# A four-layer Mamba and convolution kernel: half 1 of each image taken first, the next image's first steps moved ahead, column matmuls issued in one run, and three smaller edits

## The chip, the cores and the metric

The kernel runs on one core of one Trainium2 chip. Its metric is the device time of one execution in microseconds (us). Before the change the median of three runs is 5528.93 us (5525.22 to 5535.81). The profiled execution took 5550.92 us, with a span of 5548.9 us and a mean granted TensorE clock of 0.898.

Engines are named as in the profile: PE is TensorE (PEld its weight loads), DVE is VectorE, ACT is ScalarE, POOL is GpSimd, SP is the queue engine that issues most loads. Each takes its own instructions in order.

## The reference, cut to what matters

Input and output are `x` of shape (8, 384, 32, 32), float32: eight images, 384 channels, 1024 pixels. Four layers follow each other.

```python
# layer 0, per image (B=8, C=384, L=1024 pixels as a sequence, 16 states per channel)
xn = rmsnorm(x)                                   # over channels
def mamba(x):                                     # once forward, once on the flipped sequence
    u, z  = split(x @ in_proj.T)
    u     = silu(causal_conv1d(u, 4 taps))
    dt, Bm, Cm = split(u @ x_proj.T)
    delta = softplus(dt @ dt_proj.T + b)
    h     = exp(delta*A) * h + delta*u*Bm         # step by step along the sequence
    y     = sum(h * Cm) + u*D
    return (y * silu(z)) @ out_proj.T
g = (mamba(xn) + flip(mamba(flip(xn)))) * scale_mod
x = x + res_scale * (g + sigmoid(dwconv3x3(xn)) * xn)
# layer 1: bn -> 1x1 conv -> dwconv3x3 -> bn -> 1x1 conv, + x          (gives x1)
# q, k, v = 1x1 conv(x1); phi(t) = exp(0.5*(2t - t*t)) on q and k; 8 heads
# kv = k'v; z = 1/(q . sum(k)); out = (q kv) z; proj, + x1             (gives x2)
# layernorm over channels, 384 -> 1536 -> 384 MLP with gelu, + x2
# layers 2 and 3: depthwise convolutions up to 13x13 with folded branches, a 1x1 conv, gelu
```

The change touches layers 0 and 1 only.

## The kernel before, in words

An image's 1024 pixels are handled as two halves `h` of 512, its channels as three chunks of 128 (`c` or `m`). Layers 0 and 1 are written as generators, in `_layers01`:

- `front(b)` is layer 0 up to the scan: load `xi` (L578), squares and norm (`sq`, then `rsqrt_mean` with the matmuls `ms_s`, `ms_b`), `xn` (L585), in-projection (`in`, `uz`), the 3x3 local branch (`lc`, `lg`; the sigmoid is L615, `local` is L617 to L620), the 4-tap convolution (`c`, `uc`), `xd`, and the deltas (`dt`, `dl`, `deltas`), which are stored to DRAM.
- `scan(b)` is the recurrence. It has twelve units: direction `d`, half `h` (0, 1 forward, then 1, 0 backward), chunk `c`. A unit has four rounds `r`. In each round and for each of two pairs of channel groups, ACT makes the decay `da` (L771), DVE makes `du` in PSUM (L776) and runs two scans into `hs` (L788), POOL multiplies `hs` by Cm (L797), and PE sums the states with four 128x32 matmuls, one per strip of 32 output rows (`sums`, L733), two of them from each `hs` tile, into `acc`. At the end of a unit `acc` goes to `yf_d`, or in the backward direction DVE multiplies it by `zr` and POOL stores `g_d` (L745). The last thing stored for an image is thus `g` of half 0.
- `layer1(b)` is layer 1: load `xx` and `g` (L878, L879), out-projection `op` (L885 adds it to `xx`), first 1x1 conv (`h`, `hh`, L893) with a store and a reload of the image, 3x3 conv (`dw`), second 1x1 conv (`c2`, L910 to L917), keys and values (`kp`, `vt`, `kvs`, L929 to L955), queries (`qp`), the normaliser (`den`, `rz`, `rzb`, L1002 to L1020), projection (`pj`), layer norm (`mu`, `ln`, `var`), MLP (`mf` L1055, `hm` L1057, `mo` L1059). `last` (L1065) stores the result to `x2_d`.

The driver at the end steps `scan(b)` 48 times for each image, and between the steps advances `front(b + 1)` and `layer1(b - 1)` so that their yielded costs stay in the proportion 90 to 325 and are used up at the last round (L1087 to L1115). What is left then is run before the next image. After image 7's scan, `layer1(7)` runs alone, and then layers 2 and 3 (`conv`, L282).

The written order is not the final one: a scheduler orders each engine's instructions by priority and by when it expects their inputs, and so may put other instructions between two that stand together in the source. `defer` and `tick` hold back a DVE step by one or more rounds; `force` runs it early (L931).

Full matmuls of 384x128 by 512 go through `dense` (L500). Products with 32 output rows go through `col32` (L507): four matmuls for the four column strips of the array. Shared buffers: seven `a6` tiles (128x3x512: `xi`, `xn`, `uc`, `xx`, `g`, `hh`, `dw`, `qp`, `pj`, `ln`), nine `t2` tiles (128x512), eight `hs`, four `da`, four `w`; in PSUM one `acc`, one `du`, two `mm` (`psum`) and three `mo` (`long_psum`).

Of the kernel before, what the change touches and what calls it, by code (L numbers as in the profile page):

```python
# [1 line left out]

# [12 lines left out]
P = 128  # L15
# [3 lines left out]
W = 32  # L19
# [18 lines left out]
N_REP, N_DA, N_HS = 6, 4, 8  # L38
TP = H * (KP // 2)
# [335 lines left out]
def _layers01(tc, nc, B, xv, x2_d, dram, ident, mean_w, eps5, eps6, one, half, minus1, vec, bns, bnt,  # L375
# [12 lines left out]
    with ExitStack() as ctx:  # L388
# [45 lines left out]
        selt = const(sel, [P, 32], "selt")  # L434
        neg_a = const(alog, [P, NG, NR], "neg_a")
        nc.scalar.activation(neg_a, neg_a, AF.Exp)
        nc.vector.tensor_scalar_mul(neg_a, neg_a, -1.0)
        mask = const(headmask, [PR, PR], "mask")
        m8 = const(mask8.rearrange("(k p) e -> p k e", p=P), [P, NC, 32], "m8")
        nc.scalar.dma_start(wdt[32:64, :], mask8_t)  # L440
# [42 lines left out]
        def defer(n, fn):  # L483
            e = [n, fn]
            late.append(e)
            return e

        def force(e):
            if e in late:
                late.remove(e)  # L490
                e[1]()
# [15 lines left out]
        def col32(ps, lhs, rhs, taps):  # L507

            for i in range(taps):
                for j in range(4):  # L510
                    nc.tensor.matmul(  # L511
                        ps[32 * j : 32 * j + 32, :], lhs(j, i), rhs(j, i),
                        start=(i == 0), stop=(i == taps - 1), skip_group_check=True,
                    )
# [17 lines left out]
        def conv3(t_d, slot, h, c, taps, name, psum=psum):  # L532

            ims = []
            for j in range(4):
                im = sp.tile([P, 18 * (W + 2)], FP, tag="im", name=f"{name}_i{j}", bufs=N_IM)
                src = bass.AP(
                    t_d.tensor, t_d[slot, 32 * (4 * c + j), 16 * h * (W + 2)].offset,
                    [[IMG, 32], [1, 3], [1, 18 * (W + 2) - 2]],
                )  # L540
                nc.sync.dma_start(im[:96, 0 : 18 * (W + 2) - 2], src)
                ims.append(im.rearrange("p (h w) -> p h w", w=W + 2))
# [3 lines left out]
                lambda j, i: ims[j][:96, i : i + 16, 0:W], 3,  # L546
# [25 lines left out]
        def front(b):  # L572

            xn = []
            for h in range(2):
                cols = bass.ts(h, HALF)
                xh = a6(f"xi_{b}_{h}")
                nc.sync.dma_start(xh, xv[b][:, :, cols])  # L578
                sqs = [t2(f"sq_{b}_{c}_{h}") for c in range(NC)]
# [29 lines left out]
            for h in range(2):  # L609
                for c in range(NC):  # L610
# [4 lines left out]
                    nc.scalar.activation(lc, ps, AF.Sigmoid, bias=vec("dw_b0", c))  # L615

                    def local(h=h, c=c, lc=lc, xr=xr):  # L617
                        nc.vector.tensor_mul(rows(lc), rows(lc), xn[h][c])
                        nc.vector.scalar_tensor_tensor(xr, lc, rs, xr, ALU.mult, ALU.add)
# [6 lines left out]
            for h in range(2):  # L626
                cols = bass.ts(h, HALF)
                ucs = [a6(f"uc_{b}_{h}_{d}") for d in range(2)]
                for c in range(NC):
                    uts = []  # L630
                    for j in range(4):
# [5 lines left out]
                        nc.sync.dma_start(ut[:, 0 : HALF + 3], src)  # L637
                        uts.append(ut)
                    for d in range(2):
# [3 lines left out]
                            lambda j, i: uts[j][:, 3 * d : 3 * d + HALF], 1,  # L643
                        )
                        nc.scalar.activation(ucs[d][:, c, :], ps, AF.Silu, bias=vec("conv1d_b", c))  # L645
# [4 lines left out]
                for k in range(NC):  # L650
                    for d in range(2):
                        nc.tensor.matmul(
                            ps[64 * d : 64 * d + 64, :], wx[:, k, :], ucs[d][:, k, :],
                            start=(k == 0), stop=(k == NC - 1), skip_group_check=True,
                        )
# [31 lines left out]
        def scan(b):  # L687
# [36 lines left out]
            def sums(k, r, hs, acc, y0, zt):  # L724
# [7 lines left out]
                for j in range(4):  # L732
                    nc.tensor.matmul(  # L733
                        acc[32 * j : 32 * j + 32, :], selt, hs[j // 2][:, bass.ts(j % 2, HALF)],
                        start=False, stop=(r == NR - 1), skip_group_check=True,
                    )
                if r < NR - 1:
# [12 lines left out]
            for k, (d, h, c) in enumerate(units):  # L750
                cols = bass.ts(h, HALF)
                second = k % (2 * NC) >= NC
                for r in range(NR):
# [9 lines left out]
                    hs = []  # L763
                    way = slice(None) if d == 0 else slice(None, None, -1)
                    end = HALF - 1 if d == 0 else 0
                    for i in range(2):
# [30 lines left out]
                        nc.gpsimd.tensor_mul(  # L797
                            pairs(t), pairs(t), bct[r][:, 1:2, :].to_broadcast([P, 2, HALF])
                        )
                        hs.append(t)  # L800
                    late.append((k, r, hs, acc, y0, zt))
# [70 lines left out]
        def layer1(b):  # L872

            xx = []
            w = wtile(outproj_t, f"wo_{b}")
            for h in range(2):
# [3 lines left out]
                xx.append(xh)  # L880
# [7 lines left out]
            for h in range(2):  # L888
# [17 lines left out]
            res = [[], []]  # L906
            for h in range(2):
                for m in range(NC):
                    ps = long_psum(f"c2_{b}_{m}_{h}")
                    dense(ps, w, m, dws[h])  # L910
                    t = t2(f"c2_{b}_{m}_{h}")
                    nc.scalar.activation(t, ps, AF.Identity, bias=biasc[:, m, :])

                    def residual(o=xx[h][:, m, :], t=t):
                        nc.vector.tensor_add(o, o, t)

                    res[h].append(defer(1, residual))  # L917
# [11 lines left out]
            for t in range(L // P):  # L929
                h, q = divmod(t, HALF // P)  # L930
                for e in res[h]:  # L931
                    force(e)
                pix = xx[h][:, :, q * P : (q + 1) * P]
                kp, vt = t2(f"kp_{b}_{t}"), t2(f"vt_{b}_{t}")
                for w, dst in ((wk, kp), (wv, vt)):
# [7 lines left out]
                    else:  # L943
                        vv1 = vt[:, : C + NPR].rearrange("p (a e) -> p a e", e=PR + 1)
                        nc.gpsimd.memset(vv1[:, :, PR : PR + 1], 1.0)
# [47 lines left out]
            qps, rzs, xns = [], [], []  # L993
# [8 lines left out]
            for h in range(2):  # L1002
                den = long_psum(f"den_{b}_{h}")
                for k in range(NC):
                    nc.tensor.matmul(
                        den[32:64, :], ksv[:, k, :], qps[h][:, k, :], start=(k == 0), stop=(k == NC - 1)
                    )
                rz = t2(f"rz_{b}_{h}")
                nc.scalar.activation(rz[32:64, :], den[32:64, :], AF.Ln, bias=eps6[32:64])
                nc.scalar.activation(rz[32:64, :], rz[32:64, :], AF.Exp, scale=-1.0)  # L1010
                rzs.append(rz)
                yield 3
            for h in range(2):
                for k in range(NC):
                    ps = long_psum(f"rzb_{b}_{h}_{k}")
                    nc.tensor.matmul(
# [192 lines left out]
```

## Time and profile before

| stretch of the span | us | PE busy | DVE busy | ACT busy | POOL busy | clock |
|---|---|---|---|---|---|---|
| scan of image 0 | 192.5 to 671.4 | 298.65 | 423.42 | 288.56 | 330.10 | 0.68 |
| scan of image 1 | 671.4 to 1203.4 | 464.41 | 452.69 | 349.51 | 339.10 | 0.93 |
| scan of image 3 | 1759.3 to 2311.6 | 463.26 | 433.63 | 349.74 | 333.97 | 0.90 |
| scan of image 5 | 2861.5 to 3387.2 | 455.92 | 426.98 | 358.83 | 331.18 | 0.93 |
| scan of image 7 | 3929.9 to 4405.0 | 379.62 | 399.99 | 259.96 | 315.76 | 0.90 |
| layer 1 of image 7, layers 2 and 3 | 4405.0 to 5548.9 | 1045.75 | 161.57 | 173.10 | 176.20 | 0.95 |

Scans end one after another, so an image's stretch is the time from the end of the last scan product of the image before to the end of its own. The front of the next image and layer 1 of the one before run inside it. Busy time is the union of an engine's instructions in the stretch. A row with two busy columns near its length has no room; a row with none has waits.

Groups of instructions that the change touches, from the table of groups by line:

| line | engine, what | count | mean ns |
|---|---|---|---|
| L733 | PE, `acc` sums (two records per matmul) | 3072 | 657 |
| L511 | PE, `dw`, `lc` (two records per matmul) | 1152 each | 611, 656 |
| L615 | ACT, sigmoid | 48 | 688 |
| L618, L619 | DVE, the local branch | 48 each | 1470, 958 |
| L912 | ACT, `c2` bias | 48 | 679 |
| L915 | DVE, residual | 48 | 1006 |
| all | ACT, table loads | 755 | 1283 |

### The profile page before, as it was taken

To read this page: it belongs to the slowest core of one execution; us is meant where nothing else is said; L and a number is where in the kernel's file an instruction comes from. 1 tells how busy PE (TensorE), PEld (TensorE's weight loads), DVE (VectorE), ACT (ScalarE), POOL (GpSimd) and SP (SyncE) were. 2 spreads that over 40 slices of the span, in tenths; PEclk is the share of its full clock that TensorE was granted. 3 is DMA by queue.
4 is the path that set the end of the run, shared out by engine and by line. 5 is a ranking of instruction groups with operands and counts; after the bars stand their busy time and mean duration, and the time that the engine had idled before them with its cause. 6 is when DMAs were issued, how large, how long until landed. Compare 5 with 4: busy or idle time off the path is not lost. (4 is left out here: it accounts for less than half of the span.)

```text
span 5548.9 us, 57079 instructions
## 1 busy us (share of the span) xinstructions
PE 4603.1 (83%) x19360; PEld 2057.3 (37%) x19360; DVE 3614.0 (65%) x3679; ACT 2906.8 (52%) x3902; POOL 2888.6 (52%) x1603
## 2 busy tenths in 40 slices
PE   5665589868996899689978987898698799899899
PEld 1221133323332333233323322333233243697598
DVE  1598997967787778687977896788788601111211
ACT  1565546774686368646774776477546422001211
POOL 3476676646665666555755674567566500110133
PEclk8776699989998999899989998999898899999999
DMA  9755585787578755864565576557644622466676
GB/s 322 236 178 165 185 258 185 213 217 227 187 234 200 232 168 191 190 200 152 196 214 175 158 213 180 179 172 212 171 142 144 110 87 57 109 166 170 185 166 149
DMA packets 528251, 1012.11 MB, mean 182 GB/s; under 512 B 60616, under 2 KB 196248, under 8 KB 527960
## 3 DMA queue, kind: packets, MB, share of 16 engines
q1 hardware_dynamic: 387952, 665.99, 39.6%
q0 software_dynamic: 71136, 248.53, 17.4%
q10 hardware_dynamic: 68872, 93.95, 5.2%
q8 instruction: 154, 2.52, 0.2%
q14 instruction: 137, 1.12, 0.1%
HBM read 763.86 MB, written 288.36 MB: 190 GB/s over the span
## 5 line engine op out<-in xcount | busy, mean ns | idle before, releaser
L797 POOL TENSOR_TENSOR hs<-hs,bct 128x1024 f32<-128x1024 f32 x768 | 2377.3, 3097 | 1078.2 <-DVE hs L788 600.5
L771 ACT ACTIVATE da<-dlt,neg_a 128x512 f32<-128x512 f32 x1536 | 1031.0, 714 | 759.0 <-DVE hs L788 716.1
L788 DVE TENSOR_TENSOR_SCAN hs<-da,carry,du 128x512 f32<-128x512 f32 x768 | 946.5, 1268 | 327.8 <-ACT da L771 161.5
L776 DVE TENSOR_TENSOR du<-vr,bct 128x1024 f32<-128x1024 f32 x768 | 1057.2, 1377 | 85.8 <-DMA vr<-v_d 50.2
L788 DVE TENSOR_TENSOR_SCAN hs<-da,du 128x512 f32<-128x512 f32 x768 | 898.6, 1207 | 80.2 <-ACT da L771 36.2
L733 PE MATMUL acc<-hs,selt 128*32 128x512 f32 x3072 | 668.9, 657 | 263.6 <-POOL hs L797 235.4
L1059 PE MATMUL mo<-hm,w 128*128 128x512 f32 x1152 | 569.4, 636 | 89.5 <-ACT hm L1057 64.0
L502 PE MATMUL mf<-ln,w 128*128 128x512 f32 x1152 | 549.8, 619 | 38.9 <-ACT uc L645 27.9
L771 ACT ACT_TABLE_LOAD x295 | 378.5, 1283 | 21.0 <-issue 7.1
L1059 PEld LDWEIGHTS mo<-hm,w 128*128 128x128 f32 x1152 | 216.1, 198 | 432.2 <-issue 243.5
L733 PEld LDWEIGHTS acc<-hs,selt 128*32 128x32 f32 x3072 | 111.7, 113 | 671.6 <-POOL hs L797 395.5
L502 PEld LDWEIGHTS mf<-ln,w 128*128 128x128 f32 x1152 | 216.7, 196 | 361.6 <-issue 296.5
L502 PE MATMUL in<-xn,win 128*128 128x512 f32 x576 | 295.8, 645 | 27.1 <-ACT phi_k L869 26.0
L316 PE MATMUL cv_b<-xt_b,toep 128*64 128x256 f32 x2688 | 304.7, 388 | 14.2 <-DVE xt_b L298 14.2
L316 PE MATMUL cv_a<-xt_a,toep 128*64 128x256 f32 x2688 | 305.5, 389 | 9.4 <-DVE xt_a L298 9.4
L316 PEld LDWEIGHTS cv_b<-xt_b,toep 128*64 128x64 f32 x2688 | 282.6, 199 | 36.8 <-issue 16.1
L316 PEld LDWEIGHTS cv_a<-xt_a,toep 128*64 128x64 f32 x2688 | 282.7, 199 | 31.9 <-issue 11.2
L502 PE MATMUL op<-g,wo 128*128 128x512 f32 x288 | 151.0, 679 | 160.0 <-issue 90.0
L511 PE MATMUL dw<-dw_i,t3b 96*32 96x512 f32 x1152 | 211.6, 611 | 39.0 <-DMA dw_i<-h_d 38.6
L511 PE MATMUL lc<-lc_i,t 96*32 96x512 f32 x1152 | 199.8, 656 | 38.3 <-issue 29.0
L1057 ACT ACTIVATE hm<-mf,biasf 128x512 f32<-128x512 f32 x192 | 130.9, 687 | 176.9 <-PE mf L502 175.3
L298 DVE COPY xt_b<-xt_b 64x2480 f32<-64x2480 f32 x24 | 38.2, 1594 | 263.1 <-DMA xt_b<-xp_d 263.1
(185 smaller groups left out, 5287.9 us busy)
## 6 DMA issues: line engine op xcount, KB each, us to landing
dlt<-dl_d SPq DMA_DIRECT2D x384, 256.0 KB, 4.4
vr<-v_d SPq DMA_DIRECT2D x384, 256.0 KB, 4.8
bct<-bc_d SPq DMA_DIRECT2D x256, 256.0 KB, 4.3
ut<-u_d SPq DMA_DIRECT2D x192, 257.5 KB, 5.1
lc_i<-xn_d SPq DMA_DIRECT2D x192, 228.8 KB, 5.3
dw_i<-h_d SPq DMA_DIRECT2D x192, 228.8 KB, 4.5
tp_d<-g_d POOLq DMA_DIRECT2D x64, 672.0 KB, 7.1
w<-w_d SPq DMA_DIRECT2D x64, 576.0 KB, 5.6
```

Source lines behind the costliest of these rows:

```text
L298: nc.vector.tensor_copy(half1[:, :, 0 : XL - 1], half0[:, :, 1:XL])
L316: nc.tensor.matmul(ps[2 * H * e : 2 * H * (e + 1), 0:BW], tp[:, 2 * (g % (GB // 2)) + e, :, :, t].rearrange("p c j -> p (c j)"), rhs, star ...
L502: nc.tensor.matmul(ps, w[:, k, m * P : (m + 1) * P], rhs[k] if isinstance(rhs, list) else rhs[:, k, :], start=(k == 0), stop=(k == NC - 1),)
L511: nc.tensor.matmul(ps[32 * j : 32 * j + 32, :], lhs(j, i), rhs(j, i), start=(i == 0), stop=(i == taps - 1), skip_group_check=True,)
L733: nc.tensor.matmul(acc[32 * j : 32 * j + 32, :], selt, hs[j // 2][:, bass.ts(j % 2, HALF)], start=False, stop=(r == NR - 1), skip_group_ch ...
L771: nc.scalar.activation(da[:, bass.ts(j, HALF)], dlt[:, bass.ts(j, HALF)], AF.Exp, scale=neg_a[:, g, r : r + 1],)
L776: nc.vector.tensor_mul(pairs(du), pairs(vt), bct[r][:, 0:1, :].to_broadcast([P, 2, HALF]),)
L788: nc.vector.tensor_tensor_scan(t[:, s][:, way], da[:, s][:, way], du[:, s][:, way], k_c if second else 0.0, ALU.mult, ALU.add,)
L797: nc.gpsimd.tensor_mul(pairs(t), pairs(t), bct[r][:, 1:2, :].to_broadcast([P, 2, HALF]))
L1057: nc.scalar.activation(hm, ps, AF.Gelu, bias=biasf[:, NC * i + f, :])
L1059: nc.tensor.matmul(acc[m], wb[:, f, m * P : (m + 1) * P], hm, start=(i == 0 and f == 0), stop=(i == FF // C - 1 and f == NC - 1),)
```

## The change

1. **Second half first.** `layer1` makes `op` and `h` for half 1 before half 0, since half 1's `g` was finished three units earlier.
2. **First steps ahead.** Eight rounds before the end of an image's scan, four steps of the front after the next (both loads of `x`, norm, `xn`) and one of the coming `layer1` (weights, `xx` and `g` of half 1) are issued. New `yield 0`s make these separate steps. The planner's costs become 100 and 310.
3. **Column products in one run.** `together` gives the products after the first a high priority and keeps them in program order, and ties the first one to everything that the run reads, for the scheduler's order alone.
4. **Residual from PSUM.** DVE adds the `c2` product, its bias and the residual in one operation that reads PSUM; the ACT copy and the held-back addition go, and `force` with it.
5. **Normaliser side by side.** `den` of both halves lies in two column strips of one PSUM tile and `rz` in one tile, so the matmuls of the two halves can run together, and ACT does both logarithms and then both exponentials. `rzb` alternates between the halves.
6. **Sigmoid from tanh.** sigmoid(x) = (1 + tanh(x/2))/2, with the halves folded into `dwh` and `rsh`. DVE's multiply becomes (t + 1) * xn.
7. The ones column of `vt` is copied by ACT from a constant instead of being set by POOL.

```diff
+AHEAD = 5000
...
+        behind = mybir.DependencyInfo(mybir.DependencyClass.NoSync, mybir.DependencyReason.DATA)
+        def together(products, made):
+            for i, product in enumerate(products):
+                if i == 0:
+                    first = product()
+                    for m in made:
+                        tc.add_manual_dep(first.ins, m.ins.name, behind, reason="together")
+                else:
+                    with tc.high_priority(AHEAD):
+                        tc.keep_in_program_order(product())
+        def col32(ps, lhs, rhs, taps, made):
+            together([ ... for i in range(taps) for j in range(4)], made)
...
                 nc.sync.dma_start(xh, xv[b][:, :, cols])
+                yield 0
...
-                    nc.scalar.activation(lc, ps, AF.Sigmoid, bias=vec("dw_b0", c))
+                    nc.scalar.activation(lc, ps, AF.Tanh, bias=dwh[:, c, :], scale=0.5)
                     def local(h=h, c=c, lc=lc, xr=xr):
-                        nc.vector.tensor_mul(rows(lc), rows(lc), xn[h][c])
-                        nc.vector.scalar_tensor_tensor(xr, lc, rs, xr, ALU.mult, ALU.add)
+                        nc.vector.scalar_tensor_tensor(
+                            rows(lc), rows(lc), one, xn[h][c], ALU.add, ALU.mult
+                        )
+                        nc.vector.scalar_tensor_tensor(xr, lc, rsh, xr, ALU.mult, ALU.add)
...
-            def sums(k, r, hs, acc, y0, zt):
+            def sums(k, r, hs, made, acc, y0, zt):
-                for j in range(4):
-                    nc.tensor.matmul(
-                        acc[32 * j : 32 * j + 32, :], selt, hs[j // 2][:, bass.ts(j % 2, HALF)],
+                together([
+                    partial(
+                        nc.tensor.matmul, acc[32 * j : 32 * j + 32, :], selt,
+                        hs[j // 2][:, bass.ts(j % 2, HALF)],
                         start=False, stop=(r == NR - 1), skip_group_check=True,
                     )
+                    for j in range(4)
+                ], made)
...
-            for h in range(2):
+            for h in (1, 0):
                 xh, gh = a6(f"xx_{b}_{h}"), a6(f"g_{b}_{h}")
...
-                    t = t2(f"c2_{b}_{m}_{h}")
-                    nc.scalar.activation(t, ps, AF.Identity, bias=biasc[:, m, :])
-                    def residual(o=xx[h][:, m, :], t=t):
-                        nc.vector.tensor_add(o, o, t)
-                    res[h].append(defer(1, residual))
+                    o = xx[h][:, m, :]
+                    nc.vector.scalar_tensor_tensor(o, ps, biasc[:, m, :], o, ALU.add, ALU.add)
...
-                        nc.gpsimd.memset(vv1[:, :, PR : PR + 1], 1.0)
+                        nc.scalar.copy(vv1[:, :, PR : PR + 1], ones)
...
+            den, rz = long_psum(f"den_{b}"), t2(f"rz_{b}")
+            ats = [slice(32, 64), slice(96, 128)]
+            for k in range(NC):
+                for h, at in enumerate(ats):
                     nc.tensor.matmul(
-                        den[32:64, :], ksv[:, k, :], qps[h][:, k, :], start=(k == 0), stop=(k == NC - 1)
+                        den[at, :], ksv[:, k, :], qps[h][:, k, :], start=(k == 0), stop=(k == NC - 1),
+                        skip_group_check=True,
                     )
...
+            for k in range(NC):
+                for h, at in enumerate(ats):
                     ps = long_psum(f"rzb_{b}_{h}_{k}")
+                    nc.tensor.matmul(ps, wdt[at, bass.ts(k, P)], rz[at, :], start=True, stop=True)
                     nc.vector.tensor_mul(qps[h][:, k, :], qps[h][:, k, :], ps)
-                yield 3
+                yield 1
...
-                work.append([front(b + 1), 90, 0])
+                work.append([fronts[b], 100, 0])
-                work.append([layer1(b - 1), 325, 0])
+                work.append([seconds[b - 1], 310, 0])
...
+                if i == rounds - 8:
+                    for gen, n in ((fronts[b + 1 : b + 2], 4), (seconds[b : b + 1], 1)):
+                        for _ in range(n):
+                            for g in gen:
+                                next(g)
```

## The prediction

> **What bounds the kernel now.** I read the page's busy shares first, then cut the span into the eight images of the scan (an image ends where the last `hs` product of its twelve units ends on POOL), then one image into its units.
>
> ```profile
> PE 4603.1 (83%) x19360; PEld 2057.3 (37%) x19360; DVE 3614.0 (65%) x3679; ACT 2906.8 (52%) x3902; POOL 2888.6 (52%) x1603
> ```
>
> No engine is full, and the shares mix stages. The scan runs from 192.5 to 4405 us; the rest is one lone layer 1 (to 4760 us) and the convolutions, where TensorE is 99% busy and which the diff leaves alone. Image 4 of the scan, one row per unit (columns: length; PE, PEld, DVE, ACT, POOL busy; granted clock; DMA share; GB/s):
>
> ```profile
> 2311.60:2383.80 72.20, 36.84 (x155) 15.23 (x154) 46.58 (x56) 37.01 (x52) 33.85 (x32) 0.76 0.82 188
> 2416.20:2446.70 30.50, 25.82 (x147) 7.40 (x147) 29.16 (x33) 9.92 (x16) 25.49 (x9) 0.94 0.67 199
> 2501.60:2551.80 50.20, 48.06 (x186) 22.55 (x186) 31.86 (x27) 31.01 (x45) 27.11 (x14) 1.00 0.22 76
> 2718.70:2753.60 34.90, 34.90 (x118) 12.51 (x111) 31.89 (x26) 33.06 (x40) 25.86 (x11) 1.00 0.68 226
> 2794.00:2861.50 67.50, 64.45 (x197) 22.88 (x197) 36.72 (x33) 61.26 (x67) 31.37 (x21) 0.99 0.57 194
> ...
> sum 549.90, PE 466.03 PEld 174.40 DVE 432.19 ACT 365.67 POOL 332.95; mean PE 38.84 PEld 14.53 DVE 36.02 ACT 30.47 POOL 27.75
> ```
>
> A unit can't be shorter than DVE's own scan work (30.5 us, unit 2). Some units are bound by DVE, some by PE (4 and 9; unit 11 by PE and ACT together). The first unit is bound by nothing: 72.2 us with DVE at 46.6 and PE at 36.8. The first units of images 1 to 7 last 58.4, 68.8, 72.6, 72.2, 52.6, 69.1 and 59.8 us, mean 64.8. The timeline of PE and SP at that boundary, and the list of waits, say why:
>
> ```profile
> 2323.51 1.13 PE L666 MATMUL dt<-xd,wdt 24*128 24x512 f32 x4
> 2355.64 3.50 PE L502 MATMUL op<-g,wo 128*128 128x512 f32 x4 [31.01 <-issue]
> 2359.07 0.86 PE L555 MATMUL ms_s<-sq,mean_w 128*32 128x128 f32 x24
> 2346.67 0.37 SPq L879 DMA_DIRECT2D g<-g_d  x1
> ```
>
> ```profile
> PE op L502 <- issue: 90.0, 3, 31.0
> PE op L502 <- DMA g<-g_d: 70.1, 5, 32.6
> PE ms_b L564 <- ACT ms_r L561: 62.6, 15, 21.3
> DVE xx L885 <- PE op L502: 105.6, 17, 31.7
> DVE xn L585 <- PE ms_b L564: 65.9, 10, 18.8
> ```
>
> Layer 1 begins with half 0, whose `g` is the last thing the scan writes. PE takes its instructions in order, so the next image's norm matmuls (`ms_s`, `ms_b`) and scan sums queue behind it, and DVE behind those (18.3 us in image 4). Part of the 31 us is the store: `g_d` is issued at 2326.5, after three `x2_d` stores (16.8 us to landing in the page's list of issues), and `g` is loaded only 20 us later.
>
> **What the Trainium skill says.** "TensorEngine Tiling (Array Packing)", Key Properties: "Tiles operate independently". The trace agrees: a complete column group of `acc` (8 records, 4 matmuls) takes 1.06 us, and two of its records alone take 1.02, so a group cut in two pays a second pass. "ScalarE: Activation LUTs", Table sets, puts tanh in the exp set, and the same page prices a load at 1283 ns plus a drain; the trace has 1283 ns, and `da` starts 0.01 us after it, so no drain is added here. "SBUF — State Buffer", SBUF: two separate sides: DVE operations with two SBUF inputs share a port pair with GpSimd and block. The trace agrees: L915 (both inputs in SBUF) has median 691 but mean 1006 ns, while L885 with one input from PSUM has mean 742.
>
> **The change part by part.** Counts come from the instruction order of the two builds, durations from the trace.
>
> *Second half first, and steps ahead.* Half 1's `g` was written by unit 8. In the new order PE has, between the last `acc` product and the first matmul that needs half 0, the last `mo` (2.84), one or two `in` (2.84 each) and `op` of half 1 (3 x 2.84 = 8.5): about 14 us that don't wait for it. In images 1 to 6 the `g_d` store also stands ahead of at least two of the three `x2_d` stores, so it lands after some 4 us instead of 20. From the end of the last `acc`: DVE has about 8 us of scans ahead of `zr`, then issue and landing 5, load 7: 20 us against 14 of work, so about 6 us of PE wait remain instead of 31. The norm of the next image moves eight rounds up, into units 9 to 11. DVE's boundary waits in the scan are 105.6 - 40.9 (in the lone tail) + 65.9 = 130 us; I take 110 as saved. Queued behind the remaining wait: `op` of half 0 and one `acc` group, so DVE can wait for `acc` again; `hs` has eight buffers, two rounds' slack. The a6 tiles limit the move: `g` of half 0 takes the buffer of `ln` of the image before, free once its last `mf` is done, which the new order has ahead of the boundary. The tail after 4405 us: PE waits 28.1 us for `g`; `op` of half 1 now fills 8.5.
>
> *Column products in one run.* Of 384 `acc` groups 222 stood unbroken, now 358. Counted as 0.95 us passes over the order, `acc` needs 502 before and 403 after; `lc` 160 and 145; `dw` 164 and 170; `c`, `xd` 296 and 294. That is 110 passes, and the normaliser's two halves side by side (`den`) save 24 more: 134 x 0.95 = 127 us of PE. In image 4 the units with PE at 95% or more (4, 5, 9, 11) are 197 of 550 us, so I count about 55 us of it (43%, some units being mixed). The cost: the first product is placed only after both `hs` products.
>
> *Residual from PSUM.* Removes 48 ACT operations (0.68 us, 33 us) and a step of the chain; DVE's 48 go from mean 1006 to the 742 of L885: 13 us. PE then waits for DVE to free the bank instead of ACT; `mo` has three, and nothing needs that bank within two `c` groups, so nothing.
>
> *Sigmoid from tanh.* The 43 loads in front of L615 go, and others move: 755 loads become 691, 64 x 1.283 = 82 us of ACT. L618 becomes the form of L619: mean 1470 to 958, 24 us of DVE. ACT is bound only in unit 11, with PE, where I have counted PE: nothing extra. DVE's 13 + 24 = 37 us count in units DVE bounds (1, 2, 6, 7, 8, 10: 225 of 550): 15 us.
>
> *Ones by ACT.* Removes 64 POOL memsets (0.1 us each) that queue behind POOL's 3.1 us products, and adds 64 tiny ACT copies. Nearest row: 243 ns for 128x48 (16 us), at worst the 468 of L946 (30 us), beside an ACT that waits 716 us for DVE. PE waits 37.4 us for `vt` by this tile's answer; I take 10. *rzb order, new constants*: nothing, a dozen small operations at the start, under the first loads.
>
> Sum: 110 + 55 + 15 + 10 + 12 (tail: 8.5 and three `den` passes) = 202. 5528.9 - 202 = 5327.
>
> **The rivals.**
> A, *moved, not removed*. Per unit the new order gives PE 31, 62, 51, 21 us in units 8 to 11, where the same count had 16, 36, 35, 60 before: the pile moves from 11 to 9 and 10. If the wait for `g` stays at 15 us (half of 31) and crowding costs 10 us an image, 202 - 7x8 - 7x10 = 76 are saved: 5450. For it: `g` is still the scan's last product. Against: those 14 us of work.
> B, *PE is the bound throughout*. Then all of 127 counts, with PE's boundary waits: 62 + 70 for `op` and 63 + 49 for `ms_b`, `ms_s` (244), less 6 x 7 left, plus 8.5: 338. 5190. For it: PE is 85% busy in an image. Against: units of 30.5 us bound by DVE.
> C, *slower*. Each group now waits on PE until POOL's second product is done. At half a product (1.55 us) for 384 groups, half of it in units that PE bounds, it costs 298 us: 5327 + 298 = 5625. For it: PE already waits 235.4 us for `hs` at L733. Against: the run is placed after the product, with other matmuls ahead of it.
>
> **How the numbers follow.** Forecast 0.58, A 0.20, B 0.14, C 0.08. The time is the forecast's. The range reaches over A and to just short of B, 5200 to 5470. Faster takes the forecast, A and B less 0.01, same 0.02, slower 0.07.
>
> **What would show it.** First units of images 1 to 7 near 49 us (now 64.8); the PE wait for `op` in the scan down from 132 to about 45 us; unit 11 near 36 us and units 9 and 10 near 60 and 50; PE busy down by about 110 us or more; table loads 691; no DVE wait for ACT's `c2`; images 1 to 6 at 515 to 522 us instead of 526 to 556. It is wrong if the first unit stays above 60 us, if PE's wait for `hs` at the new run grows by over 100 us, or if DVE starts to wait for the loads that stand behind `g` in SP's queue.

## The result, and the profile after

The changed kernel took **5355.93 us** (median of 4 runs, 5353.65 to 5363.4) beside 5532.37 us for the kernel before on the same chip: **0.9685 of before, interval 0.9668 to 0.9702**. The forecast was 5327 us, 29 us too low, with a range of 5200 to 5470. In the profiled executions the span went from 5548.9 to 5351.9 us; the 197 us between them are placed below, and what the forecast's sum got wrong lies inside them.

The page after, first part:

```profile
PE 4510.2 (84%) x19360; PEld 2032.3 (38%) x19360; DVE 3602.4 (67%) x3684; ACT 2796.1 (52%) x3854; POOL 2892.9 (54%) x1539
```

PE's busy time fell by 93 us and ACT's by 111 us, DVE's by 12. Table loads fell from 755 to 691. None of this says where the time came from, so here is image 4 of the scan again, one row per unit (length; PE, PEld, DVE, ACT, POOL busy; clock; DMA share; GB/s). The rows are units 0, 2, 4, 9, 10 and 11:

```profile
2238.00:2285.90 47.90, 37.88 (x104) 14.96 (x97) 44.22 (x49) 20.97 (x32) 25.89 (x18) 0.93 0.81 158
2313.90:2344.30 30.40, 24.45 (x123) 6.04 (x122) 28.21 (x32) 14.21 (x21) 25.40 (x9) 0.83 0.73 222
2398.00:2431.10 33.10, 31.52 (x148) 15.47 (x150) 29.66 (x24) 24.95 (x45) 26.48 (x9) 1.00 0.43 138
2598.80:2656.90 58.10, 53.87 (x164) 19.20 (x168) 37.28 (x33) 49.73 (x56) 30.33 (x19) 0.94 0.59 193
2656.90:2711.20 54.30, 48.70 (x187) 19.69 (x188) 41.74 (x39) 47.98 (x58) 34.88 (x26) 0.91 0.73 221
2711.20:2746.80 35.60, 33.04 (x96) 12.93 (x98) 33.80 (x30) 29.93 (x35) 28.20 (x11) 1.00 0.67 229
```

Unit 0 went from 72.2 to 47.9 us and unit 11 from 67.5 to 35.6, while units 9 and 10 grew from 34.9 and 40.4 to 58.1 and 54.3: PE and ACT are both nearly full in them, which is where unit 11's pile now lies. Unit 4 lost 17 us: PE, which bounded it, has 16.5 us less to do there, in part because work has moved to other units (148 records of PE instead of 186). Unit 2 is DVE's own scan and did not move.

The timeline of PE, POOL and SP at this boundary:

```profile
2244.07 2.74 PE L505 MATMUL in<-xn,win 128*128 128x512 f32 x6
2248.61 7.99 PE L505 MATMUL op<-g,wo 128*128 128x512 f32 x18 [1.80 <-DVE xx L1090]
2263.10 5.29 PE L505 MATMUL op<-g,wo 128*128 128x512 f32 x6 [6.50 <-DMA g<-g_d]
2248.19 0.58 POOL L772 DMA_DIRECT2D g_d<-zr  x1
2250.56 0.36 SPq L907 DMA_DIRECT2D g<-g_d  x1
```

The `x` counts are records, two for each matmul, so x18 is the `op` of one half. Before, PE stood 31.01 us ahead of the `op` of half 0. Now `in` and the `op` of half 1 run in that time, and 6.50 us are left. The store of `g` was issued at 2248.19 and the load could start at 2250.56, 2.4 us later instead of 20. The list of waits after:

```profile
PE op L505 <- DMA g<-g_d: 98.9, 7, 18.5
DVE xx L914 <- PE op L505: 86.4, 11, 22.3
PE ms_b L582 <- ACT ms_r L579: 50.2, 14, 8.7
DVE xn L604 <- PE ms_b L582: 50.3, 15, 16.6
```

98.9 us of waits for `g` remain, 81.2 of them inside the scan (the rest is the lone layer 1 of image 7). The single waits, at the starts of images 2 to 7, are 17.7, 18.3, 6.5, 2.5, 18.5 and 17.7 us: image 4, shown above, is one of the two good boundaries, and image 5 the other.

From here on one table carries most of the reading: mean length of the groups of units over images 1 to 6, in us, cut at the ends of POOL's `hs` products. The last two rows belong to runs that are described further down.

| kernel | unit 0 | 1, 2 | 3 to 5 | 6 to 8 | 9, 10 | 11 | image | image 7 |
|---|---|---|---|---|---|---|---|---|
| before | 65.6 | 62.0 | 136.6 | 135.2 | 78.0 | 65.8 | 543.1 | 475 |
| changed | 47.6 | 63.1 | 126.0 | 128.5 | 112.4 | 36.0 | 513.6 | 453 |
| changed, again (`c_after`) | 50.4 | 63.6 | 125.3 | 129.0 | 115.7 | 36.0 | 520.1 | 459 |
| before, other order (`b_320`) | 69.9 | 61.3 | 137.6 | 138.0 | 110.5 | 37.3 | 554.7 | 471 |

Six images save 29.5 us each (177), image 7 saves 22, and the rest of the span loses 2 (up to the end of image 0 it is 7 us longer, after image 7 it is 5 shorter). Per image, unit 0 gives 18.0, units 3 to 8 give 17.3, units 1 and 2 take 1.1 back and units 9 to 11 together 4.6. These shares are good to some microseconds only: the two profiled executions had mean granted clocks of 0.898 (before) and 0.905. `c_after`, the same changed kernel on another chip at 0.898, saves 23.0 us an image against the same row: unit 0 gives 15.2, units 3 to 8 give 17.5, and units 9 to 11 take 7.9 back.

### The profile page after: what moved, and what is told of

It is laid out like the page before. It is cut to its first block, busy times and chain, and to the rows that moved or that the text cites. A ratio compares the mean times of both kernels' runs of the same rounds, so it can differ in the third digit from the quotient of the medians.

```text
span 5351.9 us, 56759 instructions
## 1 busy us (share of the span) xinstructions
PE 4510.2 (84%) x19360; PEld 2032.3 (38%) x19360; DVE 3602.4 (67%) x3684; ACT 2796.1 (52%) x3854; POOL 2892.9 (54%) x1539
## 5 line engine op out<-in xcount | busy, mean ns | idle before, releaser
L803 DVE TENSOR_TENSOR du<-vr,bct 128x1024 f32<-128x1024 f32 x768 | 1042.9, 1358 | 50.6 <-DMA vr<-v_d 35.7
L522 PE MATMUL acc<-hs,selt 128*32 128x512 f32 x2304 | 588.2, 679 | 149.5 <-POOL hs L824 149.5
L517 PE MATMUL acc<-hs,selt 128*32 128x512 f32 x768 | 440.5, 668 | 81.2 <-POOL hs L824 63.7
L318 PEld LDWEIGHTS cv_b<-xt_b,toep 128*64 128x64 f32 x2688 | 282.7, 199 | 37.2 <-issue 16.6
L1093 POOL DMA_DIRECT2D x_d<-xx x48 | 55.8, 1168 | 352.4 <-DVE xx L1090 351.7
L505 PE MATMUL op<-g,wo 128*128 128x512 f32 x288 | 146.4, 662 | 103.2 <-DMA g<-g_d 98.9
```

The lines of the kernel that those rows point to most:

```text
L318: nc.tensor.matmul(ps[2 * H * e : 2 * H * (e + 1), 0:BW], tp[:, 2 * (g % (GB // 2)) + e, :, :, t].rearrange("p c j -> p (c j)"), rhs, star ...
L505: nc.tensor.matmul(ps, w[:, k, m * P : (m + 1) * P], rhs[k] if isinstance(rhs, list) else rhs[:, k, :], start=(k == 0), stop=(k == NC - 1),)
L517: first = product()
L522: tc.keep_in_program_order(product())
L803: nc.vector.tensor_mul(pairs(du), pairs(vt), bct[r][:, 0:1, :].to_broadcast([P, 2, HALF]),)
L1093: nc.gpsimd.dma_start(x2v[m, :, h * (H // 2) : (h + 1) * (H // 2), PADW + b * (W + PADW) : PADW + b * (W + PADW) + W,], rows(o),)
```

## The experiments

Ratios are to the kernel before, measured beside each run, with 95% intervals. The runs were made on different chips (the kernel before took 5532 us beside the changed kernel, 5561 to 5564 us beside the experiments), so ratios are compared between chips, not times. Where a profile of an experiment is set against the changed kernel on a chip of the same speed, that is `c_after`.

### Undoing the order at the boundary

Half 0 first and nothing ahead (`u_order`), and half 1 first but nothing ahead (`u_ahead`); both return to the old planner's costs. The first two lines, which stand once for `op` and once for `h`, are in `u_order` alone:

```diff
-            for h in (1, 0):
+            for h in range(2):
...
-                work.append([fronts[b], 100, 0])
+                work.append([fronts[b], 90, 0])
-                work.append([seconds[b - 1], 310, 0])
+                work.append([seconds[b - 1], 325, 0])
-                if i == rounds - 8:
-                    for gen, n in ((fronts[b + 1 : b + 2], 4), (seconds[b : b + 1], 1)):
...
```

> The changed kernel with half 0 first again, no steps ahead, and the planner's old costs 90 and 325; all else as changed. Theory (the image boundary was the largest part): the first units of images 1 to 7 go back from a mean of 48 us to 62 or more, PE again idles 25 to 30 us there for g, and the time is 5356 plus 110 to 140, so 5466 to 5496. Rival (the shorter PE work of the column runs carried the gain, and a wait at the boundary is made up for later in the image): under 5400.

> The changed kernel with half 1 still first, but no steps ahead and the planner's old costs. Theory: op of half 1 covers 8.5 us of the wait for g, but its own loads and the next image's norm (ms_s, ms_b with their ACT steps) stand at the boundary again: first units near 57 us, time 5420 to 5450. Rival 1 (the order of the halves alone does it): 5360 to 5375. Rival 2 (half 1 first is worth nothing without the loads ahead): as the kernel with half 0 first, 5466 or more.

Measured: `u_order` **0.9938** (0.992 to 0.9955), `u_ahead` **0.9961** (0.9948 to 0.9974). Most of the gain is gone in both, and they are nearly equal: half 1 first brings nothing that shows by itself. The list of waits of `u_ahead`:

```profile
PE op L505 <- DMA g<-g_d: 87.4, 7, 16.0
DVE xx L914 <- PE op L505: 56.4, 12, 20.3
```

Its wait for `g` is shorter than the changed kernel's, and still its unit 0 lasts 67.9 us (`u_order` 68.6) with DVE busy for 47 of image 4's 74 us. So the turned halves do not empty the first unit without the early steps; whether the early steps would do it without the turned halves wasn't tried. This result does not hang on the drawn order, to which the next sections come: in all runs of this document the kernels without early steps have a mean first unit of 65.6 to 69.9 us (before, `b_320` and these two), and those with them one of 38.9 to 52.7.

The two kernels do not show what the early steps crowd. The early norm does stand in unit 10 of the changed kernel, and units 9 and 10 take 87.7 and 91.7 us together in the two kernels, 112.4 in the changed one, unit 11 62.2 and 60.9 against 36.0. But `b_320`, which has no early steps, has 110.5 and 37.3: another planner's cost alone moves the pile out of unit 11. And units 9 to 11 together take 149.9 and 152.6 us without the early steps, 148.4 with them.

### Undoing the column runs

```diff
-            for i, product in enumerate(products):
-                if i == 0:
-                    first = product()
...
-                    with tc.high_priority(AHEAD):
-                        tc.keep_in_program_order(product())
+            for product in products:
+                product()
```

> The changed kernel with the column products issued one by one in source order, without priority and without the tie to all inputs. By the instruction order 212 of 384 acc groups stand unbroken instead of 358, and PE needs 106 passes of 0.95 us more, 101 us. Theory (43% of them in units that PE bounds): 5356 + 45 to 60, so 5401 to 5416. Rival B (PE is the bound throughout): about 5455. Rival C (the run makes PE wait for hs, and so costs something): under 5356.

Measured: **0.9937** (0.992 to 0.9953). PE is busy for 4631.9 us against 4510.2. Units 3 to 8 take 272.7 us an image instead of 254.5, as they should when PE bounds some of them; unit 0 takes 52.7 us, 5 more than in the changed kernel and 2 more than in `c_after`, with waits for `g` of 137.9 us in all. The direction is that of the forecast; the size is more than twice the 45 to 60 us expected, and not clean, for the reason that the controls give below.

### Undoing the small parts

All four at once (`u_small`: sigmoid, ACT's `c2` copy, ones by POOL, `den` apart), and then the residual (`u_res`), the sigmoid (`u_tanh`) and the pair of `den` and ones (`u_dv`). The edits are the "+" and "-" lines of the change for these parts, turned round; for the residual:

```diff
-                    nc.vector.scalar_tensor_tensor(o, ps, biasc[:, m, :], o, ALU.add, ALU.add)
+                    nc.scalar.activation(t, ps, AF.Identity, bias=biasc[:, m, :])
+                    def residual(o=xx[h][:, m, :], t=t):
+                        nc.vector.tensor_add(o, o, t)
+                    res[h].append(defer(1, residual))
```

> The changed kernel with sigmoid, the ACT copy of c2, POOL's memset of the ones and the separate normalisers back; order, steps ahead and column runs as changed. Theory: 15 (DVE port) + 10 (memset) + 5 (den and rzb) = 30 us more, 5386. Rival (73 more table loads, 94 us of ACT, with 33 us of c2 copies are on the path): 5356 + 60 to 100. Rival (nothing of it is on the path): 5356 within 10.

> The changed kernel with only the ACT copy of c2 and the later addition back. The order of the other instructions stays as it was (9679 of 9682 on PE). ACT gets 48 copies of 0.68 us, and each kv step waits for one more link. Theory of the prediction: DVE's port sharing alone, 5 to 15 us, a ratio to the kernel before of 0.970 to 0.972. Rival (the four small edits are a real 180 us, and this is the one on the path of c2 and kv, where that kernel lost 12 us an image): 0.98 to 0.99.

> The changed kernel with only the sigmoid back: 82 table loads more by the instruction order, 105 us of ACT. Theory of the prediction: ACT has room, only the DVE form counts, 10 us, ratio 0.970. Rival 1 (units 9 and 10 are now bound by PE and ACT together, so table loads count there): 60 to 100 us, ratio 0.979 to 0.986. Rival 2 (any edit makes the scheduler draw another order, worth 1 to 2% either way): like the kernel with only the planner's cost changed.

> The changed kernel with only the normaliser's halves apart again and POOL's memset of the ones: 18 more PE passes (17 us), 64 memsets of 0.1 us on POOL. Theory: 15 to 20 us, ratio 0.971 to 0.972. Rival (another order is drawn, 1390 of PE's 9682 instructions stand elsewhere): over 0.98.

Measured: `u_small` **1.0006** (0.9995 to 1.0017), `u_res` **0.9751** (0.9735 to 0.9766), `u_tanh` **0.9807** (0.9794 to 0.9821), `u_dv` **0.9976** (0.9967 to 0.9984).

`u_small` missed all three of its expectations: the whole gain is gone, though the order of the halves, the early steps and the column runs are in place. Its first units stay short (44.2 us), and the time is lost elsewhere: units 1 to 5 take 210.7 us against 188.9 in `c_after`. `u_dv` has the same pattern (44.9 and 205.4).

`u_res` is the clean one: all but 3 of PE's 9,682 instructions keep their order, and it costs 0.66% (0.51% against `c_after`), some 28 to 37 us, where the forecast had counted about 5 (13 us of DVE at its share of bound units). Its list of waits has

```profile
DVE xx L951 <- ACT c L948: 129.7, 14, 56.6
```

against 126.6 us of waits for PE's `c` in the changed kernel, so the wait only changed its name. The time is in the unit where the `c2` products stand: unit 3 takes 52.7 us in the mean of images 1 to 6 against 49.5 in `c_after`, with ACT busy for 38.1 instead of 29.7 us there in image 4. No other unit differs by more than some 1 us.

`u_tanh` has 773 table loads instead of 691, 105 us of ACT, and pays 1.2% (some 68 us), but not where ACT is short: against `c_after`, units 6 and 8 get 9.1 and 6.0 us longer and units 9 to 11 together 6 shorter. `u_dv` makes no sense as a sum: `den` taking 43.5 us of PE instead of 28.3, and 64 memsets of 0.1 us cannot cost 2.9% (160 us). Together the single undos come to 2.5 (order), 2.5 (runs), 0.7 (residual), 1.2 (sigmoid) and 2.9%, 9.8% in all, for a change that brought 3.15%. Something else moves when one part is taken out.

### The control: the same instructions in another order

```diff
-                work.append([seconds[b - 1], 310, 0])
+                work.append([seconds[b - 1], 305, 0])
```

> A control: the changed kernel with the planner's cost for layer 1 at 305 instead of 310, and nothing else. The same instructions, in another order (1476 of PE's 9682 stand elsewhere), PE passes 4485 instead of 4482. Theory (what counts is the work and the moves at the boundary, not the drawn order): ratio 0.967 to 0.972. Rival (the time depends on the drawn order as much as on any one edit): outside 0.962 to 0.977.

Measured: **0.9587** (0.9572 to 0.9602), a point better than the changed kernel and outside the band. One planner's cost decides between the two: the list of instructions is that of the changed kernel (but for 702 table loads instead of 691, which follow from the order), but 1,476 of PE's stand elsewhere. The same was done to the kernel before:

```diff
-                work.append([layer1(b - 1), 325, 0])
+                work.append([layer1(b - 1), 320, 0])
```

> The kernel before with nothing altered but the planner's cost of the second layer, 320 instead of 325: the same instructions, with 1,839 lines of difference in the order on PE. It measures what another draw of the order is worth in the kernel before. Theory: the order that the planner and the scheduler happen to draw is worth one or more per cent in any of these kernels: outside 0.995 to 1.005, on either side, within 0.97 to 1.03. Rival: only the new arrangement, with its crowded units 9 and 10, is so sensitive, and the kernel before is not: 0.996 to 1.004.

Measured: **1.0102** (1.0084 to 1.0121). So a draw of the order was worth about one per cent in either kernel, in one draw each, and the rival (only the new arrangement is so sensitive) fell. Any single undo that moves the order carries such a term. `u_dv` moves 1,390 instructions of PE; whether its 2.9% is `den`, the memsets or the draw stays open. `u_tanh` moves about as much of PE's order as the draw of 305 does (by the traces some 5,500 of 19,360 records, 5,200 in the draw), so its 1.2% cannot be told from a draw. Open is also the share of the draw in `u_order`, `u_ahead` and `u_run`, each of which costs two and a half times as much as one draw did.

One thing that the draw of 305 does is visible. Its waits of `op` for `g`:

```profile
PE op L505 <- DMA g<-g_d: 25.2, 3, 19.6
```

25.2 us, 19.6 of them in the lone layer 1, against 98.9. Inside the scan PE happens to have other work in that place at all but one boundary. That this is what 305 gains by is not shown: its first units are hardly shorter for it (47.5 us in the mean of images 1 to 7, 48.3 in the changed kernel). But it pointed to the last experiment.

### What keeps g: the changed kernel again, and the stores held back

`c_after` is the changed kernel, unaltered, on the chip of the next runs.

> The changed kernel itself, unaltered, beside the three others, so that they can be compared with it on one chip. Expected: 0.9685 of before again, between 0.966 and 0.971. If it came out beyond that, the ratios of the earlier runs, taken on other chips, could not be compared with one another to better than that shift.

Measured: **0.97** (0.9681 to 0.9719), 5399.27 us: the ratio holds from chip to chip within its interval. Here is one of its boundaries, image 4, in the timeline of PE, POOL and SP, and in the answer of the trace on the DMA of the same 28 us (40 slices: busy tenths of the 16 engines and GB/s; then the queues; then issues with us to landing):

```profile
2290.57 5.46 PE L505 MATMUL op<-g,wo 128*128 128x512 f32 x6 [21.03 <-DMA g<-g_d]
2261.79 3.47 POOL L1093 DMA_DIRECT2D x_d<-xx  x3
2268.43 0.36 SPq L907 DMA_DIRECT2D g<-g_d  x1
```

```profile
DMA  9999799975997899699798979698999959999979
GB/s 170 111 117 53 23 53 29 38 23 23 35 41 29 32 50 41 29 44 56 41 61 56 79 44 79 35 61 99 85 102 111 170 184 275 269 342 392 345 272 334
q0 software_dynamic: 233, 0.75, 52.4%
q1 hardware_dynamic: 1113, 2.10, 32.9%
g<-g_d SPq DMA_DIRECT2D x1, 768.0 KB, 22.0
```

Three `x2_d` stores of half 1 are issued at 2261.8, `g` is loaded at 2268.4, and the load lands 22.0 us later. For 17 us the DMA engines are nearly all busy and move 23 to 80 GB/s; when the stores are through, the same engines move 270 to 390. The queue of the stores (q0) holds the engines for 52.4% of the stretch with 0.75 MB, the queue of the loads for 32.9% with 2.10 MB: a byte of these stores takes the engines 4.5 times as long. It is not their queue or size: `g_d` from `zr` goes through the same queue with the same 256 KB and lands in 3.3 us in the median in this kernel, `x_d` from `xx` in 18.6, and even the first of three such stores, with no other ahead of it, takes 11 to 19 us for six of the eight images. What differs is where they write: each of the 128 partitions writes 16 separate rows of 32 floats, 128 bytes a piece. The Trainium skill, "DMA: Bandwidth & Descriptors", Why small descriptors are slow (HBM only), gives a fixed overhead per packet and per descriptor as a reason for slow short pieces.

The short rows cannot be the whole reason, since not all of these stores are slow. Microseconds from the first issue to the last landing of three, in `c_after`, by image:

| image that is stored | 0 | 1 | 2 | 3 | 4 | 5 | 6 | 7 |
|---|---|---|---|---|---|---|---|---|
| half 0 | 28.4 | 27.3 | 24.5 | 10.0 | 25.5 | 28.0 | 31.8 | 10.1 |
| half 1 | 31.2 | 27.5 | 26.9 | 12.8 | 28.4 | 27.4 | 25.8 | 8.8 |
| start in its row, bytes past a multiple of 32 | 24 | 16 | 8 | 0 | 24 | 16 | 8 | 0 |

The stores of images 3 and 7 have the same rows of 128 bytes and take about a third of the time of the others, in every kernel of this document (8.8 to 13.5 us against 21.4 to 33.8 wherever all records are there). In the source, image `b` starts 4 x (6 + 38 b) bytes into its row of 1248 bytes, and 3 and 7 are the images for which this is a multiple of 32. No run changes the padding of the rows, so the alignment is argued from the eight images and not shown by an edit. It fits the good boundary of image 5, where the stores are those of image 3: the wait for `g` is 2.5 us there (0.8 in `c_after`), and its first unit is the shortest of images 1 to 7 in both.

`v_dep` holds these stores back until half 0's `op` is added; the DVE additions that free PSUM stay where they are. The second part stands in the next image's `layer1`, after the addition of `op` (L914), whose instruction is `added`:

```diff
-                        nc.gpsimd.dma_start(
-                            x2v[...],
-                            rows(o),
-                        )
+                        store = partial(nc.gpsimd.dma_start, x2v[...], rows(o))
+                        if h == 1 and b < B - 1:
+                            held.append(store)
+                        else:
+                            store()
...
+                    if h == 0 and m == NC - 1:
+                        while held:
+                            store = held.pop(0)()
+                            tc.add_manual_dep(store.ins, added.ins.name, behind, reason="held")
```

> The changed kernel with one thing held back: the three x2_d stores of half 1 (L1093) of each image but the last are not issued at the boundary but after the last output-projection add of half 0 (L914), so that they no longer lie beside the load of g for half 0 (L907). The order of PE, DVE and ACT stays but for some 24 of 4,898 rows. Theory: in the changed kernel this load took 12 to 20 us where it takes 7 alone, because of those stores; alone it leaves the output projection waiting some 6 us at each of the boundaries that waited 18: 98.9 us of waits become 30 to 45, and 50 to 65 us go: 0.957 to 0.960 of before (0.988 to 0.991 of the changed kernel on the same chip). Rival 1: the load is slow for another reason (it reads what was just written, or other loads run beside it): waits stay near 99 us and the ratio at 0.967 to 0.971. Rival 2: the waits go, but PE and ACT have as much to do before the image ends, and the next wait takes the time: waits 30 to 45 us and a ratio of 0.964 to 0.968.

`v_dep305` is the same edit with the cost of 305.

> The same stores held back in the control whose planner's cost is 305 instead of 310 (0.9587 of before). There the output projection waited for g only 2.0, 1.5, 4.3 and 5.0 us at four boundaries within the scan, and 19.6 us at the last one. Theory: only the last boundary has something to give, 10 to 14 us: 0.956 to 0.957 of before. If it gains as much as the same edit brings to the changed kernel (over 30 us), the gain there doesn't come from the wait for g; if it loses, the later stores collide with something else.

Measured: `v_dep` **0.9611** (0.9593 to 0.9628), 5350.3 us, 49 us less than the changed kernel on this chip (0.991 of it); `v_dep305` **0.957** (0.955 to 0.9591), 5326.46 us, the fastest of all, and within the intervals no better than 305 alone. The waits of `v_dep`, and the same boundary:

```profile
PE op L505 <- DMA g<-g_d: 15.8, 3, 9.9
DVE xx L916 <- PE op L505: 24.0, 6, 14.6
2246.30 12.14 PE L505 MATMUL op<-g,wo 128*128 128x512 f32 x24 [2.92 <-DVE xx L1096]
```

The wait for `g` falls from 125.6 us (the changed kernel on this chip) to 15.8 and the load of `g` to 4.5 us to landing in the median; rival 1 is refuted. Of the 110 us of wait, 49 became time. Where the others went is in the windows of units 0 to 2 of image 4, first of the changed kernel on this chip, then of `v_dep`:

```profile
2253.20:2305.30 52.10, 29.77 (x80) 11.78 (x73) 34.18 (x42) 16.36 (x24) 27.61 (x17) 0.77 0.78 132
2305.30:2336.80 31.50, 31.50 (x108) 11.68 (x106) 30.30 (x34) 16.89 (x27) 25.11 (x8) 1.00 0.54 178
2336.80:2367.30 30.50, 24.86 (x132) 6.28 (x124) 28.91 (x33) 14.73 (x21) 25.47 (x9) 0.89 0.75 222
```

```profile
2235.70:2273.30 37.60, 34.07 (x98) 13.60 (x91) 36.31 (x42) 16.84 (x25) 25.33 (x12) 0.95 0.54 177
2273.30:2306.10 32.80, 22.96 (x59) 8.11 (x58) 29.54 (x32) 10.98 (x18) 28.12 (x13) 0.92 0.83 78
2306.10:2346.00 39.90, 34.37 (x150) 8.54 (x151) 29.12 (x32) 18.64 (x29) 25.44 (x9) 0.77 0.76 237
```

Unit 0 loses 14.5 us and unit 2 gets 9.4 longer. In unit 1 the DMA engines are now 83% busy with 78 GB/s: the stores, issued at 2277.83, lie there, and beside them another load is late. ACT's timeline and the DMA answer for 2284 to 2312 us:

```profile
2304.56 1.33 ACT L798 ACTIVATE da<-dlt,neg_a 128x512 f32<-128x512 f32 x2 [11.46 <-DMA dlt<-dl_d]
dlt<-dl_d SPq DMA_DIRECT2D x4, 256.0 KB, 16.6
```

`dlt` takes 16.6 us where 4.3 is its median over the run, ACT stands 11.46 us for it, and PE's sums behind that. Over images 1 to 6 units 1 and 2 grew from 63.6 to 69.8 us while unit 0 fell from 50.4 to 38.9. Such waits for `dlt` are not new in the run as a whole:

```profile
ACT da L798 <- DMA dlt<-dl_d: 80.8, 14, 17.8
ACT da L798 <- DMA dlt<-dl_d: 67.6, 19, 11.7
```

The first line is the changed kernel's on this chip, where the longest of them lay in unit 0 beside the wait for `g`; in the second, `v_dep`'s, they have moved to unit 1. At image 5, where the stores are the fast ones of image 3, unit 2 takes 30.5 us in both kernels. The slow stores hold the engines for about as long here as there; only a place where no load is urgent would be free, and this wasn't one. So neither the theory (50 to 65 us) nor rival 2 (PE and ACT as the next limit; waits gone, 0.964 to 0.968) has it quite: the waits went, not quite half of them became time, and what took the rest back in units 1 and 2 is, at the boundary shown, the DMA engines. `v_dep305` came out at the size expected (0.956 to 0.957), and the last boundary's wait fell from 19.6 to 10.7 us, but 0.957 and 0.9587 lie within each other's intervals, so it neither confirms nor refutes.

## Why the prediction was right, and where it was off

**Boundary, 110 us forecast.** First units of images 1 to 7 average 48.3 us (forecast near 49; they were 64.8), which makes 7 x 16.5 = 115 us. The sum is about right (94 us by `c_after`'s first units), its term for `g` is not: the step "issue and landing 5, load 7: 20 us against 14 of work" left 6 us per boundary and 45 us in all; 81.2 were measured. The store of `g` took 2.4 to 12.3 us to land at the six boundaries, near the forecast in the mean (6.7). The load was not 7 us but 12 to 21 where its landing is recorded, because the three `x2_d` stores, which the forecast had moved out from ahead of the store of `g`, then lay beside its load. The forecast had asked what the stores delay and not what they share; `v_dep` shows it.

**Units 9 and 10, about 60 and 50 forecast.** 58.1 and 54.3 in image 4; unit 11 35.6 (36 forecast). But the sum had no term for them: units 9 to 11 cost 4.6 us an image net, 28 us over six (7.9 an image in `c_after`). Rival A had 10 us an image for this. Its mechanism isn't shown: `b_320` has the pile in units 9 and 10 without any early step, and without early steps the three units take no less (`u_order`, `u_ahead`).

**Column runs 55, port 15, memset 10.** Units 3 to 8, where these three act, gave 17.3 x 6 = 104 us against 80. The parts can't be told apart on these runs except one: the residual brings 28 to 37 us instead of some 5. Its step failed where the forecast named "48 ACT operations (0.68 us, 33 us) and a step of the chain" and priced neither, only a share of DVE's 13 us: in unit 3 the copy by ACT stands in the chain from `c2` to the next products, and that unit got 3.2 us longer per image with it, 19 us over six. DVE's own price was right there: the residual (L940) takes 739 ns in the mean, forecast 742, with one operand from PSUM, and 1006 before with both in SBUF. That agrees with "SBUF — State Buffer", SBUF: two separate sides, on which the forecast drew. The 24 us of DVE for the sigmoid did not come: the first of the two operations of the local branch went from 1470 to 1253 ns in the mean, not to 958, and the second from 958 to 1146, together 1.4 us less over 48. DVE's busy time fell by 12 us in all where 37 had been counted.

**PE busy down by 110 or more.** 93 us on the page (82 in `c_after`, at the clock of the profile before). `den` gave 16 us of 23 forecast (43.9 to 28.3 us of PE), `acc` 61 of 94, `lc` 22 where 14 were counted, and `dw` took 10 more. "TensorEngine Tiling (Array Packing)", Key Properties, holds in direction: unbroken groups are cheaper. Counting whole passes overstates it.

**Tail, 12 us.** 5 us. PE waits 17.8 us for `g` there, where 28.1 less 8.5 makes 19.6; that part was right. The other three and a half were for `den`. What took 7 of these 12 us back isn't known.

**Table loads** are 691 as counted from the order, and no DVE wait for ACT's `c2` is left. **Rival C** is refuted: PE's wait of `acc` for POOL's `hs` is 149.5 + 63.7 = 213.2 us, less than the 235.4 before. **Rival B** failed on the units that DVE bounds (unit 2 of image 4: 30.5 and 30.4 us). Images 1 to 6 took 503 to 523 us, forecast 515 to 522.

Of the 29 us between forecast and result, up to 20 are no error on the change: waits were counted on a profiled execution of 5548.9 us and taken off a median of 5528.9, and the difference of the two spans, 197 us, is 5 from the sum of 202. That agreement is partly luck, since errors of 49 and 44 us cancel. Left out or counted too high were units 9 to 11 (28 us), units 1 and 2 (7), image 0 (7) and the tail (7); too low were units 3 to 8 (24), the first units (5) and image 7 after its first unit (22 less 7, 15). A draw of the order alone would have moved the result by more.

## What to carry to other kernels

Work that is moved ahead of a boundary is worth the wait it fills, less what it crowds where it lands; count both, and count the resources that the moved transfers share, not only the queue they stand in. Before the parts of a change are priced by taking them out one by one, run a control that alters the order and nothing else: here it was worth one per cent, more than some of the parts. A slow store is best placed where no load is urgent, since holding it back only changes which load it slows; and when some stores of one kind are fast and others slow, look at the addresses that they write before moving them.

## What the runs showed of the hardware that had not been expected

- Three stores of 256 KB in rows of 128 bytes hold the 16 DMA engines for some 17 us at 23 to 80 GB/s, and loads beside them take three to five times as long, on another queue: `g` 22.0 us (6.9 in the median before), `dlt` 16.6 to 21.5 (4.3).
- The same three stores take 8.8 to 13.5 us for images 3 and 7 and 21.4 to 33.8 us for the other six. Only for those two do the rows begin at a multiple of 32 bytes within the row of 1248 bytes; that this is the reason is not tested.
- The same program waited 98.9 us for `g` in one profiled execution and 125.6 us in another on another chip (clock 0.905 and 0.898): a wait that a collision of transfers makes is not a constant of the kernel.
